# Two non-local attention blocks on one core: later spreading of keys, mixed weights in five steps, theta of the first block in slots 0 and 1

## The chip, the cores and the metric

The kernel runs on one core of a Trainium2 chip. The metric is the device time of one execution in microseconds (us). The engines are named as in the profile: PE is TensorE (matmuls), DVE is VectorE, ACT is ScalarE, POOL is GpSimd and SP is SyncE. POOL and SP do no arithmetic here: they issue DMAs, POOL those that add to what is there.

## The reference

Two layers of a non-local block with the same shapes and different weights are applied one after the other to x, four images of 128 channels and 96 x 96 pixels in float32. In each layer, for every image:

```python
g_x     = maxpool2(conv1x1(x, g_w, g_b))        # 64 channels, 2304 keys
theta_x = conv1x1(x, theta_w, theta_b)          # 64 channels, 9216 queries
phi_x   = maxpool2(conv1x1(x, phi_w, phi_b))    # 64 channels, 2304 keys
attn    = softmax(theta_x^T phi_x)              # over the keys
y       = attn g_x^T
x       = batchnorm(conv1x1(y, W_w, W_b)) + x
```

## The kernel before

One image in one layer is a block, and the eight blocks run in a fixed order. A block's queries are cut into nine pairs of 2 x 512, its keys into 18 tiles of 128. A *slot* is two key tiles of one pair. In a slot PE multiplies the two tiles' keys with the pair's theta (`scores`, L684, into one of two PSUM buffers), ACT takes the exponential of each (L689, into one of five `exp` buffers), DVE adds it to the pair's running sum (L698), and PE multiplies the exps of the slot before with the values (`values`, L706, into the only `av` buffer, which ACT copies away at L713 when a pair is done). A pair has nine slots, so 648 slots make the whole kernel. Two pairs, 18 slots, are a *cycle*; slots of a cycle are counted from 0 to 17, and a step given for slot 24 falls in slot 6 of the next cycle.

All other work is written into these slots by hand. The order of every engine's instructions is the order in which the program names them (the schedule is manual), and each engine executes its own in that order. In each slot the main loop calls, in this order: scores of the first tile; `first`, if the slot has one; scores of the second tile; `second`; the adds for the two tiles, with `take` between them or behind; the values of the slot before; then the lists `squares`, `tails` and `after` of this slot.

- **Units.** The theta and keys of the next block are made by four `Unit`s, one a cycle, in eight stages at the slots `STEPS = (8, 9, 11, 12, 14, 17, 20, 23)`. A stage's matmuls (L489; the first, the split, L498) go into two PSUM banks of a pool that has only those two, and its `_sum` on DVE or ACT takes the result out. The stages form sums and differences of products of *mixed* weights (below) with sums of pixels, so that fewer matmuls are needed. `sixth_sum` is L570, L571, L574 and L575, `eighth_sum` L598, L599 and L600. Each unit's pixel sums are made by DMAs (L455 on SP's queue, L458 on POOL's).
- **Pools and keys.** `pools` lists the unit's max pools (L608), its transposes (`square`, L646) and at slot 24 `spread`: ACT writes the pooled keys into the block's key planes, one activation with the bias `centre` (L639) and two copies (L641). In a block's first unit `spread` begins with `centring`, in which DVE forms the centre from the pooled keys (L627, L628), and a copy on ACT (L637).
- **Mixed weights.** `steps_mixed` makes seven sums and differences of a layer's g, phi and theta weights in four steps, `crossed`, `lower`, `upper` and `rest`: subtractions and additions on DVE, copies between the halves of the partitions on ACT (L211 to L213, L221, L225). For layer 0 they run in slots 3 to 6 of cycle 0, through the list `after`. For layer 1 they are among 15 late steps, three a cycle at slots 1, 4 and 10 (`PREPARE`), from cycle 1 on: mixed at 1, 4 and 10 of cycle 3 and 1 of cycle 4, then five for W.
- **Theta of block 0.** Only this block has its theta made from x within the loop: in each of its cycles `thetas` takes two pairs, half of the matmuls (L295) in slot 6 and half in slot 7, into the two banks of the pool, and ACT takes them out with the bias (L678). Later blocks load theta from memory, where their units stored it.
- **Cycle 0** besides makes the last keys of block 0, at slots 0 to 5, with pools at L333, ACT's centred keys and their copy at L407 and L413, and transposes at L424, eight of them in slot 5.
- **Endings.** A pair's projection (L857, into the same two banks) is in slot 3 or 13 of the cycle after its own. Its denominators are turned by DVE (L782 to L789, slots 15 and 24), with DMAs between. The result is added to x by a DMA (L871).

The functions that the change touches, and what calls them:

Of the kernel before, what the change touches and what calls it, by code (L numbers as in the profile page):

```python
# [33 lines left out]
NP = HW // PT  # L34
# [6 lines left out]
UK = UN // 4  # L41
TB = NKT // 2
STEPS = (8, 9, 11, 12, 14, 17, 20, 23)
THETAS = 6
LOADS = (4, 12)
STORE = 3

# [16 lines left out]
def shifted_blocks(ctx: ExitStack, tc: tile.TileContext, x: bass.AP, layers, out: bass.AP, flag):  # L64
# [24 lines left out]
    nc = tc.nc  # L89
# [71 lines left out]
    class Layer:  # L161
# [40 lines left out]
        def steps_mixed(self):  # L202

            low, high = slice(0, CI), slice(CI, P)
            g, phi = slice(0, CI), slice(CI, 2 * CI)
            m = self.mixed = const.tile([P, 7, CI], F32, name=f"mixed_{self.l}")
            w, theta = self.gphi, self.theta
            sub, add = nc.vector.tensor_sub, nc.vector.tensor_add

            def crossed():  # L210
                nc.scalar.copy(m[low, 3, :], theta[high])  # L211
                nc.scalar.copy(m[high, 1:3, :], w[low].rearrange("p (i c) -> p i c", i=2))
                nc.scalar.copy(m[high, 5, :], theta[low])  # L213

            def lower():
                sub(m[low, 1, :], w[low, g], w[low, phi])
                sub(m[low, 2, :], w[low, g], m[low, 3, :])
                sub(m[low, 4, :], w[low, g], theta[low])
                sub(m[low, 6, :], m[low, 1, :], theta[low])
                add(m[low, 5, :], m[low, 6, :], m[low, 3, :])  # L220
                nc.scalar.copy(m[high, 6, :], m[low, 6, :])  # L221

            def upper():
                sub(m[high, 0, :], w[high, g], m[high, 1, :])
                nc.scalar.copy(m[low, 0, :], m[high, 0, :])  # L225
                for i in (1, 2):
                    sub(m[high, i, :], m[high, i, :], w[high, phi])
                sub(m[high, 3, :], w[high, g], w[high, phi])

            def rest():  # L230
                sub(m[high, 4, :], w[high, g], theta[high])
                sub(m[high, 5, :], m[high, 5, :], theta[high])
                add(m[high, 6, :], m[high, 6, :], w[high, phi])

            return [crossed, lower, upper, rest]

        def steps_theta(self):
            self.theta = const.tile([C, CI], F32, name=f"thetaT_{self.l}")
# [189 lines left out]
    class Unit:  # L428
# [186 lines left out]
        def pools(self):  # L615

            return [
                (11, lambda: self.pool(0, 0, 5)), (13, lambda: self.pool(1, 0, 3)),
                (16, lambda: self.pool(1, 1, 3)), (18, lambda: self.pool(0, 1, 2)),
                (19, lambda: self.pool(0, 2, 5)), (23, lambda: self.pool(1, 2, 0)),  # L620
                (21, lambda: self.square(0)), (22, lambda: self.square(1)),
                (24, self.spread),
            ]

        def centring(self):
            centre = self.blk.centre
# [5 lines left out]
        def spread(self):  # L632
            src = pooled[:, 1, :].rearrange("p (b k) -> p b k", k=32)
            planes = self.blk.planes().rearrange("p i (t k) -> p i t k", k=KT)
            if self.u == 0:
                self.centring()
                nc.scalar.copy(self.blk.centre[CI:, :], self.blk.centre[:CI, :])  # L637
            dst = planes[:, :, :, ts(self.u, 32)]
            nc.scalar.activation(dst[:, 0], src, AF.Identity, bias=self.blk.centre)  # L639
            for h in range(2):  # L640
                nc.scalar.copy(dst[ts(1 - h, CI), 1], dst[ts(h, CI), 0])  # L641
# [8 lines left out]
    class Pair:  # L650
# [211 lines left out]
        def add(self):  # L862

            here = self.runs(self.blk.xt)
            if self.number < late:
                for h in range(2):
                    nc.scalar.activation(  # L867
                        self.halves[:, ts(h, QT)], self.pss[h], AF.Identity,
                        bias=self.blk.w.shift,
                    )  # L870
                nc.gpsimd.dma_start(  # L871
                    out=here, in_=self.halves.rearrange("p (r n) -> p r n", r=2),
                    accum_op=ALU.add,
                )
            else:
                for h in range(2):
                    dst = here[:, h, :]
                    nc.vector.scalar_tensor_tensor(
                        dst, self.pss[h], self.blk.w.shift, dst, op0=ALU.add, op1=ALU.add
                    )  # L880
                self.put()
# [124 lines left out]

    after = {8: [other_cols]}
    for i, step in enumerate(ws[0].steps_mixed()):
        after[3 + i] = [step]
    for i, step in enumerate(ws[0].steps_W()):  # L1010
        after[(10, 11, 12, 13, 17)[i]] = [step]
    after[9] = [lambda: ws[1].load_gphi((nc.sync, nc.sync)), lambda: ws[1].load_theta(nc.sync)]
    after[17] += [lambda: ws[1].load_W(nc.sync)]
    steps = [lambda i=i: late_steps("gphi", i) for i in range(4)]
    steps += [lambda i=i: late_steps("theta", i) for i in range(2)]
    steps += [lambda i=i: late_steps("mixed", i) for i in range(4)]
    steps += [lambda i=i: late_steps("W", i) for i in range(5)]
    made = {}

    def late_steps(what, i):  # L1020
        if i == 0:
            made[what] = getattr(ws[1], f"steps_{what}")()
        made[what][i]()
# [34 lines left out]
    for t in range(total + 1):  # L1058
        q, s = 2 * (t // CYCLE), t % CYCLE
        even, odd = pairs[q : q + 2] if t < total else (None, None)  # L1060
        first, second, take = None, *pending
        pending = (None, None)
        unit, stage_of = stages.get(t, (None, None))
        assert unit is None or (t not in keys and second is None)
        if t in keys:
            n, i = keys[t]
            first, *pending = blocks[n].chunks(i)
        elif unit:
            first, take = unit.steps[stage_of]
            second = unit.split_rest if stage_of == 0 else None  # L1070
        elif t < total and s == THETAS and q < NP - 1:
            first, *pending = thetas(pairs[q + 1 : q + 3])
        elif t == total - 1:
            second, take = even.multiply, even.add
        elif gone and s in PROJECT:
            pair = gone[PROJECT.index(s)]
            second, take = pair.multiply, pair.add
            later(t + STORE, pair.put)
        if t < total:
            now, j = divmod(t, NB)  # L1080
            if s == 0 and q:
                gone = pairs[q - 2 : q]
            if s == 0 and q < late:
                for pair, at in zip((even, odd), FOLDS):
                    for i, step in zip(at, pair.folds()):
                        later(t + i, step)
            for i, at in enumerate(LOADS):
                if s == at and NP - 1 <= q < len(pairs) - 1 - i:
                    pairs[q + 1 + i].load_theta()
            if t in loads:  # L1090
                b, i = loads[t]
                if i == 0:
                    xs[b] = new_x(b)
                load_part(b, xs[b], i, 6)
        for i in range(KB):
            if t < total:
                pairs[now].scores(j * KB + i, rowwise=stage_of == 0 and i == 1)
            if i == 0 and first:
                first()
        if second:  # L1100
            second()
        for i in range(KB):
            if t < total:
                pairs[now].add_up(j * KB + i)
            if i == (stage_of == 0) and take:
                take()
        if t == 0:
            b0.batch(FIRST - 1)
        if t - 1 in keys and t < NB:
            b0.batch(keys[t - 1][1])  # L1110
        if t:
            before, j = divmod(t - 1, NB)
            for k in ends.get(t, range(j * KB, (j + 1) * KB)):
                pairs[before].values(k)
        if t < total:
            for i, pair in enumerate(gone):
                if s == NORM[i]:
                    pair.normalise()
            for i, pair in enumerate((even, gone[1] if gone else None)):
                if pair is None:  # L1120
                    continue
                sooner = q == late and i == 0
                if sooner and s in (SOON, SOON + 1):
                    pair.turn(s - SOON)
                if s == (SOON + 2 if sooner else HALVES[i]):
                    pair.add_halves()
                if sooner and s == SOON + 2:
                    pair.invert()
            if q == late and s == 15:
                even.normalise()  # L1130
        if t == total - 1:
            odd.last_denominators()
        for i, k in squares.get(t, []):
            b0.square(i, k)
        for step in tails.pop(t, []):
            step()
        for step in after.pop(t, []):
            step()
# [323 lines left out]
```

## Time and profile before

| | |
|---|---|
| median of 3 runs | 2490.12 us (2489.57 to 2491.87) |
| the profiled execution's own time | 2488.51 us |
| its span, first to last instruction | 2486.7 us |
| granted TensorE clock | 0.999 |
| busy share of the span | PE 99%, DVE 83%, ACT 66%, POOL 30% |
| scores L684, values L706 (PE busy) | 1387.3 us, 1315.8 us |
| exps L689 (ACT busy, mean of one) | 1396.8 us, 1113 ns |
| adds L698 (DVE busy, mean of one) | 1406.9 us, 1222 ns |

The profile is of one execution. Its span leaves out 1.8 us of the time. A busy PE isn't PE at its peak: matmuls overlap in the array, and the ends of their records are modelled, so the step from one start to the next says more than a duration. Each matmul of a 64 x 64 tile stands as two records, so a slot has 16 of L684 and 16 of L706.

### The profile page before, as it was taken

The page shows a single profiled execution, that of the slowest core. Times are in us where ns is not written, and L with a number is a line of the kernel's source. Part 1 is how long each engine was busy: PE and PEld are TensorE (multiplying, and loading weights), DVE is VectorE, ACT ScalarE, POOL GpSimd, SP SyncE. Part 2 cuts the span into 40 slices and gives each one's busy share as a digit, 9 for nine tenths or more (in the row PEclk, how much of TensorE's full clock was granted, in tenths as well). Part 3 has the DMA queues.
Part 4 walks back from the last instruction along what each step waited for, and adds up shares of the span by engine and source line. Part 5 has one row for each costly group of instructions (what it writes and reads, how often), then busy time and mean ns, then how long its engine had stood idle before and what let it go on. Part 6 is the DMA issues. An engine that isn't in the chain of part 4 may idle for free.

```text
span 2486.7 us, 58096 instructions
## 1 busy us (share of the span) xinstructions
PE 2461.7 (99%) x23335; PEld 1464.3 (59%) x23335; DVE 2064.1 (83%) x2639; ACT 1643.3 (66%) x1789; POOL 755.5 (30%) x846
## 2 busy tenths in 40 slices
PE   9999999999999999999999999999999999999998
PEld 4434445666666666664333666666666666666665
DVE  7988888888788888888878888888887888877777
ACT  5666666666666666666666666666666666666665
POOL 0332333332233233333223333333322233322220
PEclk9999999999999999999999999999999999999999
DMA  5566676765466667767556776666655677644443
GB/s 181 98 101 119 124 141 108 123 111 92 87 115 120 128 127 134 136 131 134 116 93 115 124 127 125 127 122 117 114 87 99 113 131 125 121 89 84 82 82 63
DMA packets 188885, 283.85 MB, mean 114 GB/s; under 512 B 33334, under 2 KB 113344, under 8 KB 188608
## 3 DMA queue, kind: packets, MB, share of 16 engines
q0 software_dynamic: 91136, 137.68, 41.0%
q1 hardware_dynamic: 97304, 142.31, 20.5%
q8 instruction: 185, 3.03, 0.5%
q14 instruction: 92, 0.75, 0.1%
q10 hardware_dynamic: 168, 0.07, 0.0%
HBM read 54.07 MB, written 35.68 MB: 36 GB/s over the span
## 4 chain that ended last, share of the span: by engine, by line
PE 93%; DVE 4%; ACT 2%; issue 1%; DMA 0%; SPq 0%; DVEq 0%; ACTq 0%
PE sc L684 43%; PE av L706 42%; PE unit_ps L489 5%; DVE sum L698 3%; PE W_ps L857 2%; ACT exp L689 1%; PE gphi_ps L349 0%; PE unit_ps L498 0%; PE theta_ps L295 0%; ACT phi L641 0%; DVE gT L646 0%; DVE stage L599 0%; DVE stage L598 0%; DMA x<-in_x_dram 0%; ACT phi L639 0%
## 5 line engine op out<-in xcount | busy, mean ns | idle before, releaser
L689 ACT ACTIVATE exp<-sc,nshift 128x1024 f32<-128x1024 f32 x1296 | 1396.8, 1113 | 748.8 <-PE sc L684 709.2
L698 DVE TENSOR_TENSOR sum<-sum,exp 128x1024 f32<-128x1024 f32 x1151 | 1406.9, 1222 | 303.3 <-ACT exp L689 250.2
L684 PE MATMUL sc<-theta,phi 64*64 64x512 f32 x10368 | 1387.3, 590 | 12.4 <-ACT exp L689 12.4
L706 PE MATMUL av<-exp,gT 64*64 64x512 f32 x10368 | 1315.8, 589 | 0.0
L706 PEld LDWEIGHTS av<-exp,gT 64*64 64x64 f32 x10368 | 653.8, 133 | 450.6 <-issue 226.5
L684 PEld LDWEIGHTS sc<-theta,phi 64*64 64x64 f32 x10368 | 660.8, 133 | 426.9 <-issue 199.9
L458 POOL DMA_DIRECT2D sums<-x x252 | 292.6, 1409 | 482.6 <-PE unit_ps L489 304.7
L762 POOL DMA_DIRECT2D turned<-sum x140 | 115.5, 946 | 668.1 <-DMA turned<-sum 564.5
L775 POOL DMA_DIRECT2D sum<-turned x280 | 232.4, 1225 | 99.9 <-DMA sum<-turned 88.7
L871 POOL DMA_DIRECT2D x<-halves x70 | 83.9, 1199 | 371.5 <-ACT halves L867 327.6
L489 PE MATMUL unit_ps<-sums,mixed 64*64 64x384 f32 x896 | 146.5, 483 | 0.0
L696 DVE TENSOR_TENSOR sum<-exp,exp 128x1024 f32<-128x1024 f32 x72 | 88.2, 1225 | 46.8 <-ACT exp L689 46.5
L713 ACT COPY halves<-av 128x1024 f32<-128x1024 f32 x71 | 71.9, 1012 | 36.5 <-PE av L706 36.5
L846 POOL DMA_DIRECT2D halves<-halves x70 | 94.7, 1353 | 0.6 <-issue 0.4
L608 DVE TENSOR_REDUCE pooled<-stage 128x96 f32<-128x384 f32 x168 | 91.6, 545 | 0.0
L867 ACT ACTIVATE halves<-W_ps,shift 128x512 f32<-128x512 f32 x140 | 88.6, 692 | 0.0
L489 PEld LDWEIGHTS unit_ps<-sums,mixed 64*64 64x64 f32 x896 | 61.3, 133 | 39.6 <-issue 16.1
L857 PE MATMUL W_ps<-halves,WT 64*64 64x512 f32 x568 | 82.8, 590 | 0.0
L489 PE MATMUL unit_ps<-x,mixed 64*64 64x384 f32 x448 | 74.3, 483 | 0.0
L646 DVE STREAM_TRANSPOSE gT<-pooled 32x288 f32<-32x288 f32 x112 | 52.5, 469 | 2.2
L857 PEld LDWEIGHTS W_ps<-halves,WT 64*64 64x64 f32 x568 | 36.6, 133 | 24.8 <-issue 9.0
L851 DVE TENSOR_TENSOR halves<-halves 128x512 f32<-128x512 f32 x71 | 48.6, 684 | 0.0
(141 smaller groups left out, 808.3 us busy)
## 6 DMA issues: line engine op xcount, KB each, us to landing
sums<-x POOLq DMA_DIRECT2D x252, 192.0 KB, 5.9
x<-halves POOLq DMA_DIRECT2D x70, 512.0 KB, 5.7
sums<-x SPq DMA_DIRECT2D x112, 192.0 KB
turned<-sum SPq DMA_DIRECT2D x140, 128.0 KB
turned<-sum POOLq DMA_DIRECT2D x140, 128.0 KB, 3.8
halves<-halves POOLq DMA_DIRECT2D x70, 256.0 KB, 5.6
halves<-row SPq DMA_DIRECT2D x140, 128.0 KB
out_dram<-x SPq DMA_DIRECT2D x35, 512.0 KB
```

The source lines that it names most:

```text
L458: return lambda: nc.gpsimd.dma_start(out=dst(), in_=src(), accum_op=ALU.add)
L489: nc.tensor.matmul(bank[ts(c, CI), :UN], lhsT=lhsT, rhs=rhs[:, c, :], start=True, stop=True)
L608: nc.vector.tensor_reduce(pooled[:, side, ts(j, UK)].rearrange("p (h w) -> p h w", w=W // 2), self.s[:, i, :].rearrange("p (h a w b) -> p ...
L684: nc.tensor.matmul(ps[ts(c, CI), ts(h, QT)], lhsT=self.blk.keys_of(k, c, h), rhs=self.th[ts(h, CI), :], start=True, stop=True,)
L689: nc.scalar.activation(e, ps, AF.Exp, bias=nshift)
L698: nc.vector.tensor_add(self.sum, self.sum, e)
L706: nc.tensor.matmul(self.av[ts(h, CI), ts(r, QT)], lhsT=self.blk.gT[ts(r, CI), k, :], rhs=e[ts(r, CI), ts(h, QT)], start=(k == 0), stop=(k ...
L762: nc.gpsimd.dma_start(out=self.turned[ts(h, CI)], in_=self.sum[ts(h, CI), ts(h, QT)], accum_op=ALU.add,)
L775: nc.gpsimd.dma_start(out=folded()[ts(i, SQ)], in_=self.turned[ts(i, SQ), ts(k, n)], accum_op=ALU.add,)
L846: nc.gpsimd.dma_start(out=self.y, in_=self.halves[:, QT:], accum_op=ALU.add)
L857: nc.tensor.matmul(self.pss[h][ts(c, CI), :], lhsT=self.blk.w.W[ts(h, CI), ts(c, CI)], rhs=self.y[ts(h, CI), :], start=True, stop=True,)
L867: nc.scalar.activation(self.halves[:, ts(h, QT)], self.pss[h], AF.Identity, bias=self.blk.w.shift,)
```

## The change

Three edits change the order of work; no instruction is added or taken away.

1. In a block's first unit `centring` is called from the list, at slot 23 (after that slot's pool) and no longer within `spread`, and `spread` comes at slot 26 instead of 24. Other units keep slot 24.
2. `steps_mixed` has five steps. `lower` and `upper` hold DVE operations alone: the subtraction that makes entry 0 of the upper half moves into `lower`, two subtractions of `rest` into `upper`. The two copies on ACT that stood in `lower` and `upper` make a step of their own, `crossed_again`, and the addition that needs one of them is `last`. For layer 0 they run in slots 3 to 7. Layer 1 has 16 late steps: its mixed ones are at 1, 4, 10 of cycle 3 and 1, 4 of cycle 4, and each of the five for W comes one place later.
3. `THETAS` is a pair: in cycle 0 theta stays in slots 6 and 7, in cycles 1 to 3 it is in slots 0 and 1.

```diff
-THETAS = 6
+THETAS = (6, 0)
...
                 add(m[low, 5, :], m[low, 6, :], m[low, 3, :])
-                nc.scalar.copy(m[high, 6, :], m[low, 6, :])
+                sub(m[high, 0, :], w[high, g], m[high, 1, :])
 
             def upper():
-                sub(m[high, 0, :], w[high, g], m[high, 1, :])
-                nc.scalar.copy(m[low, 0, :], m[high, 0, :])
                 for i in (1, 2):
                     sub(m[high, i, :], m[high, i, :], w[high, phi])
                 sub(m[high, 3, :], w[high, g], w[high, phi])
 
-            def rest():
                 sub(m[high, 4, :], w[high, g], theta[high])
                 sub(m[high, 5, :], m[high, 5, :], theta[high])
+
+            def crossed_again():
+                nc.scalar.copy(m[high, 6, :], m[low, 6, :])
+                nc.scalar.copy(m[low, 0, :], m[high, 0, :])
+
+            def last():
                 add(m[high, 6, :], m[high, 6, :], w[high, phi])
 
-            return [crossed, lower, upper, rest]
+            return [crossed, lower, upper, crossed_again, last]
...
-                (24, self.spread),
-            ]
+            ] + ([(23, self.centring), (26, self.spread)] if self.u == 0 else [(24, self.spread)])
...
             if self.u == 0:
-                self.centring()
                 nc.scalar.copy(self.blk.centre[CI:, :], self.blk.centre[:CI, :])
...
-        after[3 + i] = [step]
+        after[3 + i] = after.get(3 + i, []) + [step]
...
-    steps += [lambda i=i: late_steps("mixed", i) for i in range(4)]
+    steps += [lambda i=i: late_steps("mixed", i) for i in range(5)]
...
-        elif t < total and s == THETAS and q < NP - 1:
+        elif t < total and s == THETAS[q > 0] and q < NP - 1:
             first, *pending = thetas(pairs[q + 1 : q + 3])
```

## The prediction

> **What bounds the kernel now.** I read the page's first lines first, then the busy time of each engine by cycle, then the list of waits, then the timeline at the places where cycles differ.
>
> ```profile
> span 2486.7 us, 58096 instructions
> ...
> PE 2461.7 (99%) x23335; PEld 1464.3 (59%) x23335; DVE 2064.1 (83%) x2639; ACT 1643.3 (66%) x1789; POOL 755.5 (30%) x846
> ```
>
> TensorE (PE) is the bound almost everywhere. What a change of order can bring is only the time in which PE stands still. To find it I cut the span into slots: each slot begins with the first of 16 score matmuls (L684), and 18 slots are a cycle. In the timeline two score groups take 1.72 us from start to start and two groups of values 1.72, so a bare slot is 3.44 us. A stage of a unit adds 0.64, the split 0.32, half a theta step or a projection 0.86. Eighteen slots with one unit (0.32 + 7 x 0.64) and two projections (1.72) come to 68.4 us. The busy times by cycle (first the stretch, its length, then each engine's busy time) for cycles 0, 1, 2, 3, 10 and 6:
>
> ```profile
> 17.68:92.64 74.96, 72.47 (x674) 30.79 (x676) 65.12 (x110) 47.57 (x59) 14.53 (x16) 1.00 0.50 116
> 92.64:164.95 72.31, 71.34 (x676) 30.79 (x672) 63.09 (x96) 47.31 (x53) 22.82 (x26) 1.00 0.61 103
> 164.95:235.96 71.01, 70.50 (x676) 32.77 (x672) 61.07 (x87) 47.18 (x52) 22.79 (x26) 1.00 0.66 123
> 235.96:308.76 72.80, 71.37 (x676) 34.70 (x672) 60.29 (x85) 48.04 (x58) 22.78 (x26) 1.00 0.66 121
> ...
> 716.36:786.66 70.30, 68.68 (x660) 44.63 (x656) 59.42 (x78) 46.25 (x51) 23.58 (x26) 1.00 0.65 117
> ...
> 447.82:516.22 68.40, 68.40 (x662) 45.11 (x658) 58.92 (x77) 45.83 (x50) 23.66 (x26) 1.00 0.66 113
> ```
>
> Cycle 6 (the last row) has PE busy for all of its 68.4 us, the length worked out: nothing is lost. Cycle 10, where a block's first unit spreads its keys, takes 1.9 us more for the same matmuls. So do cycles 5, 14, 19, 23 and 28, with 1.8 to 2.0 each: **11.65 us in all**. Cycles 1 to 3 should take 68.36 + 1.72 for theta = 70.08 and take 2.2, 0.9 and 2.8 more, 5.9 together. Cycle 0 loses 4.5, of which 3.5 in slots 6 and 7. With 0.5 in cycles 4 and 15 that is about 22.5 us, all that there is to win inside the cycles. The list of waits (total us, times, longest) names the causes:
>
> ```profile
> ACT centre L637 <- DVE centre L628: 17.3, 7, 2.6
> ...
> ACT mixed L221 <- DVE mixed L219: 5.4, 2, 3.2
> ACT mixed L225 <- DVE mixed L224: 5.3, 2, 3.4
> ...
> PE theta_ps L295 <- DVE stage L599: 2.2, 3, 1.2
> ```
>
> and the timeline (start, us, engine, line; in brackets idle time before it) shows how one of them reaches PE, ScalarE (ACT) first, then PE, in cycle 10:
>
> ```profile
> 745.10 0.19 ACT L637 COPY centre<-centre 64x1 f32<-64x1 f32 x1 [2.58 <-DVE centre L628]
> 745.32 0.54 ACT L639 ACTIVATE phi<-pooled,centre 128x288 f32<-128x288 f32 x1
> 745.89 0.87 ACT L641 COPY phi<-phi 64x288 f32<-64x288 f32 x2
> 746.78 2.12 ACT L689 ACTIVATE exp<-sc,nshift 128x1024 f32<-128x1024 f32 x2
> ...
> 747.95 1.09 PE L684 MATMUL sc<-theta,phi 64*64 64x512 f32 x8 [1.62 <-ACT exp L689]
> ```
>
> The two exps of slot 7 stand behind a copy that waits for VectorE (DVE), and slot 8's scores need the buffer that the first of these exps frees.
>
> **The skill.** Three places bear on this. "Trainium Architecture — The Big Picture", Inside one NeuronCore: each engine has its own instruction stream, and they meet only at semaphores; the trace agrees, since 1.4 us of small copies of keys cost PE nothing in cycle 6 and the wait ahead of them costs 1.9. "Perfetto Trace Analysis", Optimizing Scalar/DVE Operations: engines that aren't saturated can still cause bubbles on others; ACT is at 66% here and does. "ScalarE: Activation LUTs", What ACT_TABLE_LOAD costs: an ACTIVATE with a pointer bias takes about 280 + 0.833 N ns, and back-to-back ones overlap by about 93. For N = 1024 that is 1133; the exp row has 1113, and two in a row take 2.12 us here. I use the trace's durations.
>
> **The later spread.** DVE's centring (0.44 + 0.15 us, unchanged) is queued in slot 5 instead of 6, straight behind the last pool; the adds and the turn of slots 5 and 6 come 0.6 us later, and the adds have room: five exp buffers let them lag by more than a slot. In cycle 10 the pool ended 2.91 us into slot 6, so the centre is there by 3.5, and ACT asks for it 3.9 us into slot 8: over 7 us to spare. The wait goes. The ACT work (0.19 + 0.54 + 0.87 = 1.6 us) now follows the two split copies of slot 8, which ended 3.86 us into it (slot length 3.8). In slot 9 it therefore ends at about +1.78. The first exp, ready at +1.25, runs to 2.9, the 0.47 us stage copy to 3.3, the second exp to 4.4, which is +0.34 of slot 10. There ACT's copy of av (L713) starts at +0.39 today, when PE has finished av, so it isn't delayed. Slot 9's own scores need exps that ended in slot 8; slot 10's need the one that ends at 2.9 of 4.08. Hidden, with little to spare: 0.05 us before L713 moves, and another 0.3 before the next values wait for av (it ends at +1.40, they start at +1.72). For first units after block 1's the gain is six times, **11.65 us**; that one's is counted with cycle 1. No DMA moves, and the keys are first read cycles later.
>
> **The mixed weights.** No instruction is added but the order changes. In cycle 0 the copy L221 (slot 4's) no longer waits 2.15 us, so slot 5's exps start when their scores are ready. L225 is worse:
>
> ```profile
> 45.50 3.06 DVE L424 STREAM_TRANSPOSE gT<-stage 32x192 f32<-32x192 f32 x8
> 48.58 0.22 DVE L224 TENSOR_TENSOR mixed<-gphiT,mixed 64x64 f32<-64x64 f32 x1
> ...
> 48.84 0.24 ACT L225 COPY mixed<-mixed 64x64 f32<-64x64 f32 x1 [3.42 <-DVE mixed L224]
> ...
> 50.27 2.09 PE L684 MATMUL sc<-theta,phi 64*64 64x512 f32 x16 [2.12 <-ACT exp L689]
> ```
>
> Both copies now run after slot 6's exps; their sources were written by DVE a slot or more before. Without the first wait DVE adds exp at +2.9 of slot 5 rather than +3.95, so the two pools free the banks for theta near +1.0 of slot 6, not 2.1, when theta's second bank is wanted. What remains of 3.5 us is about 0.05: **gain 3.45**. The five upper subtractions (0.7 us) and the last add end in slot 7, before slot 8's split and slot 9 read them. In cycle 3 the same waits, 3.2 and 1.85 us, go; this is in the next sum. Layer 1's W steps move one place on, to at latest cycle 6; block 2 needs them in cycle 9. A little more DVE work falls in cycle 5, far from its limit of 83% busy. I cost that at nothing, since the split two slots later is the first to need DVE; without that cover it would be 0.5.
>
> **Theta to slots 0 and 1 (cycles 1 to 3).** At slot 6 its first half takes both banks behind slot 5's eighth stage, whose sums DVE ends 2.1 to 2.8 us into slot 6. At slot 0 it follows the sixth stage of slot 17. Its first bank is freed by the third operation, L574:
>
> ```profile
> 94.07 0.54 DVE L574 TENSOR_TENSOR stage<-stage,unit_ps 128x384 f32<-128x384 f32 x1
> ```
>
> This ends 1.97 us into slot 0 of cycle 1, and 1.39 and 1.72 in cycles 2 and 3; theta is due at 0.86. **A new wait: 1.1 + 0.5 + 0.9 = 2.5 us.** Behind it in PE's queue is the slot's second score group, behind that exp and values. The take (two of 0.69 on ACT) follows slot 1's exps to +4.43 against a slot of 4.30, and the seventh stage wants the banks 0.86 later: free. DVE gets 0.86 us more in each of slots 0 and 1, so the seventh's sums are sooner ready for slot 3's projection; it loses as much in 6 and 7, which then are as in cycle 6. POOL's accumulating DMAs of slots 5 to 8 get as much time as in cycle 6 too, and x's update at slot 3 now comes after theta has read, with the one of slot 13 landed in slot 15. SP's stores keep their slots. With the block's spread gone from slot 6 and the mixed waits from 5 and 11, cycles 1 to 3 lose 2.5 in place of 5.9: **gain 3.4**.
>
> The price of that new wait is the unsure one: nothing if DVE runs ahead in slot 17, at most 1.5 each (4.5) if all four operations were waited for.
>
> **The sum:** 11.65 + 3.45 + 3.4 = 18.5 us. The profiled execution took 2488.5 (span 2486.7 and 1.8 around it), so 2470.0 like for like; its time lies 1.6 below the runs' median of 2490.1, which gives **2471.6**.
>
> **Rivals.**
> 1. ACT's burst at slots 8 to 10 overruns its 0.37 us. For: split copies, spread, stage copy and av copy follow each other closely. Against: the row-by-row times above just fit. An overrun of 0.5 more at seven places is 3.5 us: 2475.
> 2. Theta's new wait costs what the old ones did (4.5 us and a late seventh stage): 3.4 less gained, again 2475.
> 3. Slower: the keys' copies come to wait again, now in front of L713. Slot 10's values need av, which has one buffer, so all beyond 0.37 us of lag is PE's. To lose 5 us net of the gains it takes (18.5 + 5) / 7 = 3.4 us a place, a lag of 3.7 at slot 10; the centre would have to come some 11 us later than now. Against: it is queued earlier. It would give 2495.
> 4. The waits only change their names: PE's gap in slot 7 is filled by another one just behind it, such as DVE's sums, and all stays at 2490. Against: cycle 6 does the same work without any gap.
>
> **How the numbers follow.** The case as summed 0.76, own range 2469.5 to 2473.5; rivals 1 and 2 together 0.18, to 2477; 4, 0.04; 3, 0.02. A measurement can tell about 0.2%, 5 us, from no change. Faster 0.94, within 0.04, slower 0.02. The floor is all lost time gone, 2467.6. Range 2468 to 2476.5.
>
> **What would show it.** Right: ACT's waits for centre and mixed (17.3, 5.4, 5.3 us) leave the list; cycles 5, 10, 14, 19, 23, 28 take 68.4; slot 6 of cycle 0 has no gap; theta waits for L574's bank. Wrong: idle PE at slots 8 to 11 behind ACT's exps or av, or cycles 1 to 3 above 71.5 each.

## The result, and the profile after

The changed kernel takes **2470.0 us** (median of 4 runs, 2469.84 to 2470.18) against 2489.85 for the kernel before in the same comparison. The ratio is 0.992, with a 95% interval of 0.9902 to 0.9937. Its profiled execution took 2469.84 us with a span of 2468.1; before these were 2488.51 and 2486.7, so the profiled executions differ by 18.7 us.

The first lines of the page after, and its line for the chain that ended last:

```profile
span 2468.1 us, 58124 instructions
...
PE 2457.7 (100%) x23335; PEld 1536.5 (62%) x23335; DVE 2064.3 (84%) x2639; ACT 1645.7 (67%) x1789; POOL 755.4 (31%) x846
...
PE 99%; DMA 0%; DVE 0%; ACT 0%; issue 0%; DVEq 0%
```

The engines' busy times are close to those of before (PE 2457.7 us in place of 2461.7, DVE 2064.3 in place of 2064.1), and each engine has as many instructions as before; the 28 more in the first line are semaphore instructions of the sequencers. The chain is now PE for 99% of the span; before it was PE 93%, DVE 4%, ACT 2%. (Lines after the edits have shifted numbers: scores L685, exps L690, adds L699, values L707, the copy of av L714.) Busy times by cycle, for cycles 0, 1, 2, 3, 10 and 6 as before:

```profile
18.00:89.38 71.38, 71.00 (x674) 37.19 (x676) 64.75 (x110) 47.72 (x59) 14.53 (x16) 1.00 0.51 120
89.38:160.67 71.29, 71.29 (x680) 32.79 (x676) 63.22 (x95) 47.43 (x54) 22.82 (x26) 1.00 0.62 105
160.67:231.35 70.68, 70.68 (x679) 32.43 (x675) 61.41 (x88) 47.34 (x52) 22.88 (x26) 1.00 0.67 124
231.35:302.28 70.93, 70.93 (x679) 39.51 (x675) 61.08 (x88) 48.03 (x56) 22.86 (x26) 1.00 0.67 123
707.58:775.94 68.36, 68.36 (x661) 44.30 (x656) 59.40 (x79) 46.17 (x51) 23.53 (x26) 1.00 0.68 120
439.00:507.36 68.36, 68.36 (x661) 44.22 (x657) 59.70 (x82) 45.96 (x50) 23.66 (x26) 1.00 0.65 113
```

Cycle 10 is now as short as cycle 6. So are 5, 14, 19, 23 and 28: their 11.64 us are gone. Cycle 0 takes 71.38 where 70.50 are needed (its slots 0 to 5 hold three key steps, and slot 0 has no values), so it loses 0.9 in place of 4.5. Cycles 1 to 3 lose 1.2, 0.6 and 0.85 over 70.08, 2.66 in place of 5.93. **The busy column hides these**: it says 71.29 of 71.29, because the drawn ends of theta's matmuls cover the wait. Only the length against the worked-out length shows it. PE in slot 0 of cycle 1, where theta was due 0.86 us after the first score group began:

```profile
89.38 1.40 PE L685 MATMUL sc<-theta,phi 64*64 64x512 f32 x8
90.78 1.64 PE L298 MATMUL theta_ps<-x,thetaT 64*64 64x512 f32 x5
```

Most of theta's eight matmul records start only after the operation of DVE that is shown at the end of this section. ACT's waits for `centre` and `mixed` (17.3, 5.4 and 5.3 us) are no longer in the list of waits. The 0.5 us of cycles 4 and 15 went too; what had caused them I didn't trace.

ACT in slots 8 to 10 of cycle 10, after (slot 8 begins at 737.20, slot 9 at 740.96, slot 10 at 745.03):

```profile
738.41 2.28 ACT L690 ACTIVATE exp<-sc,nshift 128x1024 f32<-128x1024 f32 x2 [1.31 <-PE sc L685]
740.60 0.53 ACT L517 COPY stage<-unit_ps 128x192 f32<-128x192 f32 x2
741.15 0.19 ACT L638 COPY centre<-centre 64x1 f32<-64x1 f32 x1
741.37 0.54 ACT L640 ACTIVATE phi<-pooled,centre 128x288 f32<-128x288 f32 x1
741.94 0.88 ACT L642 COPY phi<-phi 64x288 f32<-64x288 f32 x2
742.84 1.11 ACT L690 ACTIVATE exp<-sc,nshift 128x1024 f32<-128x1024 f32 x1
743.85 0.47 ACT L524 COPY stage<-unit_ps 128x384 f32<-128x384 f32 x1
744.21 1.13 ACT L690 ACTIVATE exp<-sc,nshift 128x1024 f32<-128x1024 f32 x1
745.39 1.01 ACT L714 COPY halves<-av 128x1024 f32<-128x1024 f32 x1
```

No bracket stands at L638: nothing is waited for. ACT works without a break from 738.41 to the end of these lines, and its copy of av starts 0.36 us into slot 10, where it started before (0.39).

In cycle 0 DVE still has its eight transposes before the upper subtractions, but nobody waits for them. DVE first, then ACT:

```profile
44.90 3.05 DVE L427 STREAM_TRANSPOSE gT<-stage 32x192 f32<-32x192 f32 x8
47.98 0.36 DVE L225 TENSOR_TENSOR mixed<-mixed,gphiT 64x64 f32<-64x64 f32 x2
...
44.86 2.35 ACT L690 ACTIVATE exp<-sc,nshift 128x1024 f32<-128x1024 f32 x2
47.23 0.24 ACT L232 COPY mixed<-mixed 64x64 f32<-64x64 f32 x1
```

And the operation that theta waits for in slot 0 of cycle 1, now L577, behind an add that ran late. It ends at 91.71:

```profile
89.05 1.22 DVE L699 TENSOR_TENSOR sum<-sum,exp 128x1024 f32<-128x1024 f32 x1
90.18 0.55 DVE L573 TENSOR_TENSOR stage<-stage,unit_ps 128x384 f32<-128x384 f32 x1
90.65 0.61 DVE L574 SCALAR_TENSOR_TENSOR stage<-unit_ps,cols_first,stage 128x384 f32<-128x384 f32 x1
91.17 0.54 DVE L577 TENSOR_TENSOR stage<-stage,unit_ps 128x384 f32<-128x384 f32 x1
```

### The profile page after: what moved, and what is told of

Read it like the earlier page. It is cut to its first block, busy times and chain, and to the rows that moved or that the text cites. A ratio compares the mean times of both kernels' runs of the same rounds, so it can differ in the third digit from the quotient of the medians.

```text
span 2468.1 us, 58124 instructions
## 1 busy us (share of the span) xinstructions
PE 2457.7 (100%) x23335; PEld 1536.5 (62%) x23335; DVE 2064.3 (84%) x2639; ACT 1645.7 (67%) x1789; POOL 755.4 (31%) x846
## 4 chain that ended last, share of the span: by engine, by line
PE 99%; DMA 0%; DVE 0%; ACT 0%; issue 0%; DVEq 0%
PE sc L685 45%; PE av L707 45%; PE unit_ps L492 5%; PE W_ps L858 2%; PE unit_ps L501 0%; PE theta_ps L298 0%; PE gphi_ps L352 0%; DMA x<-in_x_dram 0%; PE gphi_ps L298 0%; DMA gphi_nat<-in_L_conv_phi_w_dram 0%; PE den_last_ps L724 0%; DVE x L917 0%; PE W_ps L903 0%; ACT exp L690 0%; PE theta_ps L668 0%; DVE halves L896 0%
## 5 line engine op out<-in xcount | busy, mean ns | idle before, releaser
L690 ACT ACTIVATE exp<-sc,nshift 128x1024 f32<-128x1024 f32 x1296 | 1399.5, 1113 | 757.2 <-PE sc L685 715.6
L699 DVE TENSOR_TENSOR sum<-sum,exp 128x1024 f32<-128x1024 f32 x1151 | 1407.7, 1223 | 288.6 <-ACT exp L690 234.2
L685 PE MATMUL sc<-theta,phi 64*64 64x512 f32 x10368 | 1412.3, 589 | 0.4 <-ACT exp L690 0.4
L707 PE MATMUL av<-exp,gT 64*64 64x512 f32 x10368 | 1333.8, 589 | 0.0
L707 PEld LDWEIGHTS av<-exp,gT 64*64 64x64 f32 x10368 | 686.6, 133 | 425.1 <-issue 391.5
L685 PEld LDWEIGHTS sc<-theta,phi 64*64 64x64 f32 x10368 | 704.2, 133 | 389.5 <-issue 348.6
L461 POOL DMA_DIRECT2D sums<-x x252 | 299.3, 1456 | 470.5 <-PE unit_ps L492 292.9
L492 PE MATMUL unit_ps<-sums,mixed 64*64 64x384 f32 x896 | 156.7, 482 | 0.0
L492 PEld LDWEIGHTS unit_ps<-sums,mixed 64*64 64x64 f32 x896 | 76.3, 133 | 32.7 <-issue 28.4
L714 ACT COPY halves<-av 128x1024 f32<-128x1024 f32 x71 | 71.9, 1012 | 33.0 <-PE av L707 32.6
L492 PE MATMUL unit_ps<-sums,gphiT 64*64 64x384 f32 x224 | 49.9, 482 | 0.0
```

Of the source, the lines that this page charges most:

```text
L461: return lambda: nc.gpsimd.dma_start(out=dst(), in_=src(), accum_op=ALU.add)
L492: nc.tensor.matmul(bank[ts(c, CI), :UN], lhsT=lhsT, rhs=rhs[:, c, :], start=True, stop=True)
L685: nc.tensor.matmul(ps[ts(c, CI), ts(h, QT)], lhsT=self.blk.keys_of(k, c, h), rhs=self.th[ts(h, CI), :], start=True, stop=True,)
L690: nc.scalar.activation(e, ps, AF.Exp, bias=nshift)
L699: nc.vector.tensor_add(self.sum, self.sum, e)
L707: nc.tensor.matmul(self.av[ts(h, CI), ts(r, QT)], lhsT=self.blk.gT[ts(r, CI), k, :], rhs=e[ts(r, CI), ts(h, QT)], start=(k == 0), stop=(k ...
```

## The experiments

"Lost" below is a cycle's length over the length worked out for its matmuls, from the experiment's profile.

**Edit 1 alone.** On the kernel before:

```diff
-                (24, self.spread),
-            ]
+            ] + ([(23, self.centring), (26, self.spread)] if self.u == 0 else [(24, self.spread)])
...
-                self.centring()
```

> The kernel before with edit 1 alone. My theory (each of the three edits takes away its own waits): the 11.65 us of cycles 5, 10, 14, 19, 23 and 28 go, and cycle 1 falls from 2.2 us lost to 1.1, what theta's bank costs there: 12.8 us less, 2477. Rival (the three only work together, because the burst on ScalarE at slot 8 needs the room that the other edits make): less than 9 us, above 2481.

Measured: 2477.73 us, ratio 0.9949 (0.9935 to 0.9963). Cycles 5 to 28 lose nothing, and cycle 1 loses 1.1; cycle 3 still loses 2.8. The median is 12.6 us lower, close to the 12.8 expected, so the edit stands by itself. The profile also showed something that I hadn't expected. Stretches of cycle 0 (slots 6, 7 and 8), with PE's busy time first and the granted clock third from the right:

```profile
42.63:50.54 7.91, 5.79 (x48) 2.37 (x40) 6.82 (x17) 2.95 (x6) 0.83 (x1) 1.00 0.20 33
50.54:56.58 6.04, 6.04 (x41) 1.97 (x45) 5.38 (x7) 4.44 (x5) 0.00 (x0) 0.72 0.00 0
56.58:60.34 3.76, 3.76 (x45) 1.76 (x41) 1.41 (x2) 2.61 (x4) 0.00 (x0) 1.00 0.00 0
```

PE stood still for 2.1 us at the end of slot 6:

```profile
50.54 3.33 PE L682 MATMUL sc<-theta,phi 64*64 64x512 f32 x16 [2.12 <-ACT exp L687]
```

Behind this gap the granted TensorE clock was one half for 3.4 us, which makes the mean of 0.72 in slot 7. The slot took 6.04 us, where the kernel before, with the same gap and the clock at 1.00, took 4.49 in its profiled execution.

**Edit 2 alone.** On the kernel before, the five steps of `steps_mixed` and the two loops that place them, as in the change.

> The kernel before with edit 2 alone. My theory: 3.5 us of cycle 0, and in cycle 3 the 0.8 and 0.3 us of slots 5 and 12 and about half a us of slot 6, where theta's bank comes sooner: 5.2 us less, 2484.6. Rival (the copies only wait elsewhere, and theta's bank remains the later one in cycle 0): 2 us or less, 2488.

Measured: 2486.09 us, ratio 0.9985 (0.9979 to 0.9992): 4.2 us less in place of the 5.2 expected. Cycle 0 loses 0.9, as expected; cycles 1 to 3 lose 5.4. Cycle 5, however, loses 4.6 in place of 1.9. DVE, ACT and PE in its slots 5 to 8, and a stretch that holds slot 8:

```profile
395.04 0.85 DVE L157 STREAM_TRANSPOSE WT<-W_bn 32x32 f32<-32x32 f32 x4
...
403.36 0.19 ACT L640 COPY centre<-centre 64x1 f32<-64x1 f32 x1 [3.44 <-DVE centre L631]
...
406.21 2.37 PE L687 MATMUL sc<-theta,phi 64*64 64x512 f32 x9 [2.46 <-ACT exp L692]
...
406.20:411.80 5.60, 5.59 (x44) 2.90 (x48) 4.17 (x4) 3.61 (x5) 0.00 (x0) 0.70 0.37 82
```

The W transposes, one place later than before, stand in front of the first unit's centring, and ACT waits 3.44 us for it, where it waited 2.58 before; the difference is the length of the four transposes, 0.85 us. PE's gap grew from 1.6 to 2.5 us, and in this execution the clock was halved behind it (slot 8 lost another 1.7).

**Edit 2 alone, W's steps where they were.**

```diff
-    steps += [lambda i=i: late_steps("mixed", i) for i in range(5)]
-    steps += [lambda i=i: late_steps("W", i) for i in range(5)]
+    steps += [lambda i=i: late_steps("mixed", i) for i in range(4)]
+    steps += [lambda: (late_steps("mixed", 4), late_steps("W", 0))]
+    steps += [lambda i=i: late_steps("W", i) for i in range(1, 5)]
```

> The kernel before with edit 2 alone, but layer 1's five steps for W where they were, the first of them together with the last mixed step. If the 4.6 us that cycle 5 lost under edit 2 alone came from W's second transposes, moved in front of the first unit's centring on VectorE: cycle 5 loses 1.9 again, 2.7 us less than under edit 2 alone. If they came from elsewhere, cycle 5 stays above 4.

Measured: 2484.60 us, ratio 0.9978 (0.9969 to 0.9987); cycle 5 loses 2.4, half a us more than the 1.9 expected, which I didn't trace; its wait for the centre is 2.58 us again and PE's gap 1.6. So W's new place caused 0.86 us of waiting, with the half clock behind it in that execution. In the whole change it costs nothing only because edit 1 takes ACT's wait away.

**Edit 3 alone.**

```diff
-THETAS = 6
+THETAS = (6, 0)
...
-        elif t < total and s == THETAS and q < NP - 1:
+        elif t < total and s == THETAS[q > 0] and q < NP - 1:
```

> The kernel before with edit 3 alone. If the prediction's booking of 3.4 us to this part is right by itself: 2486.5. What I now hold: most of the 3.4 us belongs to the other two edits, since cycle 1's spread then waits by itself (1.9 us) and cycle 3 keeps its two waits for mixed; cycles 1 to 3 lose about 5.1 in place of 5.9: 2489, no difference that the time can tell, and theta's wait moves from slot 6 to slot 0 with 1.1, 0.5 and 0.5 us.

Measured: 2490.66 us, ratio 1.0002 (0.9994 to 1.0011). Cycles 1 to 3 lose 3.9, 0.4 and 1.8, together 6.1 where they lost 5.9. Cycle 1 is worse than I thought. With theta gone from slots 6 and 7 these are 0.86 us shorter each, so ACT comes to the spread 4.0 us after the start of slot 6 and no longer 5.4, while DVE has the centre no sooner. In cycle 1 ACT waits 3.44 us for it, where it waited 1.83 before. It is the longest in ACT's list of waits (2.6 before):

```profile
ACT centre L637 <- DVE centre L628: 18.9, 7, 3.4
```

**Theta back at slots 6 and 7**, all else as changed: `THETAS = (6, 6)`.

> The changed kernel with theta of cycles 1 to 3 back in slots 6 and 7. If theta's wait is about as long there as at slot 0 (eighth stage's sums instead of the sixth's): 1.05, 0.9 and 0.95 us in cycles 1 to 3 in place of 1.05, 0.45 and 0.45 with some tenths beside, so within 1 us of the change: 2470.5. If the booking of the prediction (3.4 us for theta's place) is right by itself: 2473.4.

Measured: 2471.05 us, ratio 0.9925 (0.9911 to 0.9938). Cycles 1 to 3 lose 1.4, 1.3 and 1.5, together 4.2, more than the 2.9 expected. Theta's place is worth 1.5 us in the profile and 1.0 in the medians.

**Spread back at slot 24, centring at 23.** On the changed kernel, `(24, self.spread)` for every unit.

> The changed kernel with the first unit's spread back at slot 24 and only the centring at 23. If the place of the centring in VectorE's queue is what counts: ScalarE asks for the centre at about +3.4 of slot 6, it is there at +3.6, the wait is 0.2 us in place of 2.6, and PE loses nothing: 2470. Rival (the two slots are what counts, the spread at slot 6 meets too much work): cycles 5, 10, 14, 19, 23 and 28 get back most of their 1.9 us: 2480 or more.

Measured: 2470.93 us, ratio 0.9925 (0.9911 to 0.9938). Cycles 10, 14, 19, 23 and 28 lose nothing. Cycle 5 loses 0.5 and cycle 1 loses 0.7 more than in the change. ACT in cycle 1 and in cycle 10:

```profile
119.88 0.19 ACT L638 COPY centre<-centre 64x1 f32<-64x1 f32 x1 [1.11 <-DVE centre L630]
...
735.07 0.19 ACT L638 COPY centre<-centre 64x1 f32<-64x1 f32 x1 [0.25 <-DVE centre L630]
```

The wait of 0.25 us is harmless. In cycles 1 and 5 DVE has layer 1's transposes to do as well, and there the two slots matter. Of the 11.66 us of cycles 5 to 28 the earlier centring alone brings 11.2; the later slot adds 0.5 in cycle 5 and 0.7 in cycle 1.

**Late spread, centring inside it.** On the changed kernel, the first unit has `(26, self.spread)` alone, and `centring` is called at its start.

> The changed kernel with the centring inside the spread at slot 26, so ScalarE asks for the centre right after VectorE is told to make it. If the order on VectorE is what counts: VectorE reaches it about 2.2 us into slot 9, ScalarE has stood since 0.2, two us later everything of slots 9 and 10 is late, some 1.7 us of PE at each of seven places: 2482. Rival (two slots later are enough): 2470 to 2472.

Measured: 2481.02 us, ratio 0.9966 (0.9954 to 0.9977). ACT waits for the centre again, seven times, 15.3 us in all:

```profile
749.41 0.19 ACT L639 COPY centre<-centre 64x1 f32<-64x1 f32 x1 [1.95 <-DVE centre L630]
```

Each of cycles 10, 14, 19, 23 and 28 loses 1.4, cycle 5 2.4, and cycle 1 5.4. In cycle 1 the clock was halved again, this time behind shorter gaps, as PE's lines and the stretch behind them show:

```profile
131.95 1.09 PE L686 MATMUL sc<-theta,phi 64*64 64x512 f32 x8 [1.43 <-ACT exp L691]
133.33 1.89 PE L686 MATMUL sc<-theta,phi 64*64 64x512 f32 x8 [0.30 <-ACT exp L691]
...
133.40:137.00 3.60, 3.60 (x20) 1.14 (x24) 2.80 (x3) 2.91 (x3) 0.89 (x1) 0.53 0.83 117
```

The later spread, with the centring still queued inside it, gives back most of what edit 1 brings.

**The key copies twice, and one of them twice.** On the changed kernel:

```diff
-            for h in range(2):
+            for h in (0, 1, 0, 1) if self.u == 0 else (0, 1):
```

> The changed kernel with the two key copies of a first unit's spread issued twice, 0.87 us more on ScalarE at seven places. If ScalarE's slack before slot 10's values is the 0.37 us of the prediction, its copy of av starts at +1.2 in place of +0.36, the values wait 0.5 us, and PE loses 3.5 us in all: 2473.5. If there is more slack than 0.9 us: 2470. If there is none: 0.87 us a place, 2476.

Measured: 2472.85 us, ratio 0.9931 (0.9917 to 0.9945). Cycles 10 to 28 lose 0.39 each. ACT, then PE, around slot 10 of cycle 10, which begins at 745.97:

```profile
742.75 1.79 ACT L642 COPY phi<-phi 64x288 f32<-64x288 f32 x4
...
746.95 1.02 ACT L714 COPY halves<-av 128x1024 f32<-128x1024 f32 x1
...
748.03 1.94 PE L707 MATMUL av<-exp,gT 64*64 64x512 f32 x16
```

The copy of av ends at 747.97 and the values, due at 745.97 + 1.72 = 747.69, start right after it. With `(0, 1, 0)`, one copy more:

> The changed kernel with one of the two key copies of a first unit's spread issued again, 0.43 us more on ScalarE at seven places. With two copies more, PE lost 0.39 us a place of the 0.87; if a fixed slack of 0.48 us stands before the values of slot 10, one copy more costs nothing (0.0 to 0.05 us a place) outside cycles 1 and 5, and the time is within 0.5 us of the change: 2470.3. If PE's loss grows in proportion from the first tenth on (no slack, 45% of the added time): 0.19 us a place, 2471.3.

Measured: 2469.81 us, ratio 0.9918 (0.9904 to 0.9931); no cycle from 5 on loses anything. So there is a fixed slack: 0.43 us more are free, of 0.87 more PE pays 0.39. It is 0.87 - 0.39 = 0.48 us wide.

**Layer 0's mixed weights in the old order**, the rest as changed: a branch for layer 0 returns the four old steps.

> The changed kernel with layer 0's mixed weights in the old order of four steps, so that only cycle 0 has its waits on ScalarE again, the 2.1 us gap of PE among them. By the waits alone: cycle 0 loses 4.5 in place of 0.9, every execution takes 3.6 us more, 2473.6, with as little spread between executions as the change has (0.3 us). If such a gap also makes the chip halve TensorE's clock in some executions: these take some 1.7 us more again, 2475.3, the others 2473.6.

Measured: 2474.18 us, ratio 0.9935 (0.9921 to 0.9948). Cycle 0 loses 4.5. The five runs took 2472.5, 2473.2, 2474.2, 2474.3 and 2474.5; two of the last three show a mean clock of 0.998, all others of this kernel and of the change 0.999. They spread over 2.0 us where the change's spread over 0.3. The profiled execution, the fastest of them, had no half clock behind its gap. This fits the second expectation in kind, though both groups lie about 1 us below the times given there and five runs are few.

**The sixth stage's sums first.** On the changed kernel, ahead of the loop over the adds:

```diff
+        if stage_of == 5 and q < NP - 1:
+            take()
+            take = None
         for i in range(KB):
```

> The changed kernel, and in cycles 0 to 3 VectorE's sums of the sixth stage (slot 17) stand ahead of that slot's adds of exp. If theta at slot 0 waits for these sums because VectorE runs late at slot 17: they end 1.2 us sooner, before theta wants its banks at +0.86, the losses of 1.06, 0.46 and 0.46 us go: 2468. Rival (VectorE's adds then hold up exp's buffers, or another wait takes the place): 2470 or more.

Measured: **2467.47 us**, ratio to the kernel before 0.9909 (0.9894 to 0.9924), the fastest of all. Cycles 1 to 3 lose 0.1, 0.0 and 0.2. DVE around slot 0 of cycle 1, which begins at 89.71:

```profile
89.37 0.55 DVE L573 TENSOR_TENSOR stage<-stage,unit_ps 128x384 f32<-128x384 f32 x1
89.83 0.61 DVE L574 SCALAR_TENSOR_TENSOR stage<-unit_ps,cols_first,stage 128x384 f32<-128x384 f32 x1
90.36 0.55 DVE L577 TENSOR_TENSOR stage<-stage,unit_ps 128x384 f32<-128x384 f32 x1
```

L577 ends 1.2 us into the slot rather than 2.3, and slot 0 takes 4.29 us, just what its matmuls need, where it took 5.03 in the change. So theta waited because the sixth stage's sums stood behind the late adds on DVE. The gain over the change is 2.5 us.

## Why the prediction was right, point by point

- **The sum.** 18.5 us were forecast for the profiled execution, 18.7 came. The three terms measured 11.66, 3.59 and 3.27, together 18.52. The 0.54 us of cycles 4 and 15, which the forecast didn't count, came on top, and 0.39 us were lost outside the cycles; that these nearly cancel is luck.
- **The median.** 2471.6 was forecast, 2470.0 measured; the medians differ by 19.85, 1.2 more than the profiled executions. The weak step is the 1.6 us between profiled execution and median, which the forecast carried over as if it were fixed. In the changed kernel that distance is 0.2. The forecast's floor of 2467.6 carries the same 1.6: the last experiment reached 2467.47 with 1.2 us still lost in cycles 0 to 3. The likely reason is the half clock, which the profiled execution of the kernel before didn't have, so that the forecast couldn't price it. Of the 59 executions of that kernel in the three comparisons of the experiments, 23 lie between 2488.2 and 2489.6 us, all with a mean clock of 0.999. Of the 36 above, 16 show 0.998. With edit 2 and W's steps unmoved, where no gap is above 1.7 us, all 11 runs show 0.999 and lie within 1.1 us. With edit 3 alone, which has gaps of 2.1 and 2.5 us, 10 of 13 show 0.998. The mean is a coarse sign, since edit 2's profiled execution shows 0.999 in spite of its stretch, and no slower execution of the kernel before was traced.
- **The spread: right to the tenth.** 11.65 forecast, 11.66 gone. The burst on ACT was worked out to end at +0.34 of slot 10; the copy of av starts at +0.36. The slack before PE pays was put at 0.37 us and measured as 0.48. Rival 1, an overrun of it, did not occur; one added copy of 0.43 would not have brought it, two did. Rival 3's mechanism is real, as the late centring shows, but its price there was 1.4 us a place, of the 3.4 that slower needed.
- **The mixed weights: right in size, wrong in its cover.** 3.45 forecast, 3.59 came. The step that failed is the nothing for W's later steps: I named the split as the first to need DVE. The first is the centring of cycle 5. Without edit 1 W's new place costs 0.86 us of waiting, and 1.7 more when the clock is halved; I had said 0.5.
- **Theta: the wait right, the booking loose.** 1.1, 0.5 and 0.9 us forecast, 1.2, 0.6 and 0.85 lost by cycle. Counted by the first score matmul of each slot, slots 0 and 1 lose 0.78, 0.19 and 0.19 of it and slots 7 to 10 the rest; counted by the fourth, slot 0 loses 1.2, 0.6 and 0.6, so cycle 3's wait was forecast too long. The gain of 3.4 stood under theta's heading though it included the block's spread and layer 1's mixed waits. Theta's place itself brings 1.5, and alone nothing. The sum was unhurt, since each was counted once. Rival 2 did not occur: cycles 1 to 3 would have lost the 5.9 us of before, and lost 2.66.
- **Rival 4**, a wait that only changes its name, held for theta alone.

The Trainium skill, "Trainium Architecture — The Big Picture", Inside one NeuronCore, says that each engine has its own instruction stream and that they meet only at semaphores. The change and the kernel with the late centring agree with it: the same 0.6 us of DVE work costs nothing or 1.4 us a place, by where it stands in DVE's stream.

## What to carry to other kernels

Where one engine is busy all through, compare each period of the schedule with the length that its work needs: the excess is what a reordering within these periods can win, and the busy column need not show it. Queue a small producer straight behind its last input, and let the consumer come when it has long been done; moving the consumer alone lost most of edit 1's gain here. Judge such edits together: edit 3 was worth nothing alone, and edit 2 had a cost that edit 1 covers.

## What the runs showed of the hardware that I had not expected

In three profiled executions a PE gap was followed by 3.4 us at half the granted TensorE clock: behind 2.1 us (edit 1 alone), behind 2.5 us (edit 2 alone), and behind 1.4 and 0.3 us with a short burst between them (the late centring, cycle 1). Each stretch cost 1.55 to 1.75 us more. "TensorE: Matmul & The Clock Gate", HAM oscillation, in the Trainium skill warns of idle gaps longer than about 3.4 us; here shorter ones did it, and the measurement decides.

The length of a gap alone doesn't tell whether it happens. The 2.1 us gap left the clock at 1.00 in the profiled executions of the kernel before, of edit 3 alone and of the old order in cycle 0. A 2.46 us gap did so with edit 3 alone, the pair of 1.4 and 0.3 us in cycle 5 of the late centring, and gaps of 1.6 us in six cycles of the kernel before. What decides it these runs don't show.
